# Layer 0's stores moved to ScalarE's queue, its loads alone on SyncE's, and four engines in the order of the source

## The chip, the cores and the metric

The kernel runs on one core of a Trainium2 chip. The metric is the time of one execution on the device in microseconds. Before the change it is 5983.85 us in the median of three executions (5970.71, 5983.85 and 6056.45).

## The reference, cut to what matters

The input is `x` of shape (4, 128, 64, 64): four images, 128 channels, 4096 positions. Four layers follow; the change concerns the first two.

Layer 0 is a selective scan (Mamba) over the 4096 positions of an image, with 256 inner channels `d` and 16 states `n`:

```
xs, zg = split(x projected twice)              # 256 + 256 channels
xc     = silu(conv4(xs) + conv_b)              # causal, 4 taps
dt, B, C = split(xc @ x_proj_w.T)              # 8 + 16 + 16
delta  = softplus(dt @ dt_proj_w.T + dt_proj_b)
h[d,n] = exp(delta[d] * A[d,n]) * h[d,n] + delta[d] * xc[d] * B[n]     # along the positions
y[d]   = sum_n h[d,n] * C[n] + xc[d] * D[d]
out    = (y * silu(zg)) @ out_proj_w.T + x
```

Layer 1 normalises this in groups, builds for each image a 4096 x 4096 matrix of zeros and ones (distance between two positions under 16), multiplies projected features with it twice, each time divided by the row's count of ones, and applies a batch norm over all images. Layers 2 and 3 are attention and a mixture of experts.

## The kernel before

**Layer 0** is tiled into chunks of 512 positions: 4 images (batches) of 8 chunks, 32 in all. The 256 x 16 pairs of channel and state lie on 128 partitions as 32 channels x 4 states, so a chunk has 16 steps. A step treats 2 x 32 channels and 4 states: `h` (0 or 1) is the half of the channels, `k` (0 or 1) the pair of 32-channel groups in it, and `q` (0 to 3) the group of states. Step `n` of a chunk has h = n // 8, q = n // 2 % 4, k = n % 2.

To bring delta and the product delta * xc, which lie as channels on partitions, to this layout, the kernel stores them to DRAM and reads them back four times over. `delta` (lines 222 to 245) makes `dl` and `dx`, and stores them in 16 DMAs of 32 rows x 512 values (64 KB) into four DRAM tiles `dd0` to `dd3`. `spread` (line 264) loads one of them as `r`, 128 partitions x 8 KB, with a source pattern of (4 copies, step 0) x (32 rows) x (2048 values). `small` (lines 212 to 220) makes B and C and stores them as `bcd`; `rates` (line 274) loads eight rows of it as `bt`, 128 partitions x 4 KB, with a source pattern of 4 x (32 copies, step 0) x 1024 values. A chunk has 4 loads of `r` and 8 of `bt`. Both have three buffers.

A step (lines 277 to 317) is:

- POOL: `db = r[dx] * bt[B]` (L289);
- ScalarE: two decays `hs = exp(r[delta] * A)` into PSUM (L295);
- DVE: two scans (L297), which need `hs` and `db`, and the `carry` of the chunk before;
- ScalarE: copy of the last column into `carry` (L300);
- DVE or, where (step number) % 3 is 1, POOL: `hc = h * bt[C]` (L302);
- PE, every second step: the sum over states, `y`, by products with `fold` (L308);
- after q = 3, DVE and POOL: `xc = (xc * D + y) * zs` (L314, L317).

Beside these steps stand, for the next chunk, the load of `xt` (L199, L201), the convolution as eight matmuls (`project`, L209, L210), `small`, `delta`, for this one the gate (`gate`, L254, L255), and for the last one the output projection (`after`, L325 to L328), which stores `x1` to DRAM.

**Layer 1** of a batch (`layer1`, from line 364) needs the whole batch of `x1`. It runs while layer 0 of the next batch does: `layer1` is a generator which yields after each portion of PE work, and the loop in lines 565 to 604 takes as many portions after each step as an even spread needs. It makes the 0/1 matrix in 8 panels `inc` (`compare`, L438, L441, and, for the mirrored part, `turn`, L451, L454, with loads `piece`, L491), multiplies by it (`edges`, L461 to L475), stores six of the panels to DRAM (L522), loads them again (`inc_v`, L533), multiplies once more (L548), and stores the result `hg` (L557). Batch 3 has no layer 0 beside it.

**The order of the work.** On each engine, instructions run one after the other. Which one comes first is decided by a scheduler, which walks through the source, takes what is ready by its own cost estimates and places it on the instruction's engine. Buffers of a pool are handed out in turn, and an instruction that needs a buffer waits until its last reader is done. All loads and stores of layers 0 and 1 are issued by SyncE, in one queue: a store that waits for its data keeps the loads behind it from being issued.

Of the kernel before, what the change touches and what calls it, by code (L numbers as in the profile page):

```python
# [38 lines left out]
class Net:  # L39
# [33 lines left out]
    def layers01(self):  # L73
        nc, tc, a = self.nc, self.tc, self.a
        DS, DR, T = 16, 8, CH
        NT = N // T
        HALF = 16.0 * 16.0 / 4.0
        TOP = 2.0**14
        with ExitStack() as ctx:
            wp = ctx.enter_context(tc.tile_pool(name="aw", bufs=1))  # L80
            hps = ctx.enter_context(tc.tile_pool(name="l0h", bufs=2, space=PSUM))
            yps = ctx.enter_context(tc.tile_pool(name="l0y", bufs=1, space=PSUM))
            ps = ctx.enter_context(tc.tile_pool(name="aps", bufs=3, space=PSUM))
# [8 lines left out]
            A = wp.tile([P, 8, DS], F32, tag="A", name="A")  # L92
# [13 lines left out]
            with tc.tile_pool(name="l0t", bufs=2) as tp0:  # L106
# [15 lines left out]

                for i in range(4):
                    nc.scalar.dma_start(
                        A[32 * i : 32 * i + 32, :, :], a["L0_conv_A_log"].rearrange("(k p) n -> p k n", p=32)
                    )
# [63 lines left out]
            def before(b, c):  # L190

                s = dict(b=b, c=c)
                t0 = c * T

                def load():
                    xt = s["xt"] = w2.tile([P, T + 3], F32, tag="xt", name="xt")
                    if c == 0:
                        nc.vector.memset(xt[:, 0:3], 0.0)
                        nc.sync.dma_start(xt[:, 3:], a["x"][b, :, 0:T])  # L199
                    else:  # L200
                        nc.sync.dma_start(xt, a["x"][b, :, t0 - 3 : t0 + T])  # L201

                def project():
                    xt = s["xt"]
                    xc = s["xc"] = w2.tile([P, 2, T], F32, tag="xc", name="xc")
                    for h in range(2):
                        pc = ps.tile([P, T], F32, tag="ps", name="ps_c")
                        for j in range(4):
                            nc.tensor.matmul(pc, wc[:, h, j, :], xt[:, j : j + T], start=j == 0, stop=j == 3)  # L209
                        nc.scalar.activation(xc[:, h, :], pc, AF.Silu, bias=vec[:, h, 4:5])  # L210

                def small():
                    xc = s["xc"]
                    xd = s["xd"] = w2.tile([40, T], F32, tag="xd", name="xd", bufs=1)
                    px = ps.tile([P, T], F32, tag="ps", name="ps_xd")
                    for h in range(2):
                        nc.tensor.matmul(px[:40, :], xpT[:, h, :], xc[:, h, :], start=h == 0, stop=h == 1)
                    nc.scalar.copy(xd, px[:40, :])  # L218
                    bcd = s["bcd"] = dp.tile([2 * DS, T], F32, tag="bcd", name="bcd")
                    nc.sync.dma_start(bcd, xd[DR:40, :])  # L220

                def delta():

                    xd = s["xd"]
                    dl = w2.tile([P, 2, T], F32, tag="dl", name="dl", bufs=1)
                    sp = w2.tile([P, 2, T], F32, tag="sp", name="sp", bufs=1)
                    for h in range(2):
                        pd = ps.tile([P, T], F32, tag="ps", name="ps_d")
                        nc.tensor.matmul(pd, dtT[:, h, :], xd[0:DR, :], start=True, stop=True)
                        nc.scalar.activation(sp[:, h, :], pd, AF.Abs, bias=vec[:, h, 5:6])  # L230
                        nc.scalar.activation(dl[:, h, :], pd, AF.Relu, bias=vec[:, h, 5:6])
                    nc.scalar.activation(sp, sp, AF.Exp, scale=-1.0)
                    nc.scalar.activation(sp, sp, AF.Ln, bias=1.0)
                    nc.vector.tensor_tensor(dl, dl, sp, ALU.add)
                    dx = sp
                    nc.gpsimd.tensor_tensor(dx, dl, s["xc"], ALU.mult)

                    dd = s["dd"] = [
                        dp.tile([32, 2, 2, T], F32, tag=f"dd{k}", name=f"dd{k}") for k in range(4)
                    ]  # L240
                    for k in range(4):
                        for i, t in enumerate((dl, dx)):
                            for j in range(2):
                                p0 = 64 * (k % 2) + 32 * j
                                nc.sync.dma_start(dd[k][:, i, j, :], t[p0 : p0 + 32, k // 2, :])

                return s, [load, project, small, delta]

            def gate(s):

                zs = s["zs"] = w2.tile([P, 2, T], F32, tag="zs", name="zs", bufs=1)
                for h in range(2):
                    pz = ps.tile([P, T], F32, tag="ps", name="ps_z")
                    nc.tensor.matmul(pz, wz[:, h, :], s["xt"][:, 3:], start=True, stop=True)  # L254
                    nc.scalar.activation(zs[:, h, :], pz, AF.Silu)  # L255

            def spread(s, k):

                r = w2.tile([P, 2, 2, T], F32, tag="r", name="r", bufs=3)
                dd = s["dd"][k]  # L260
                rows = bass.AP(
                    tensor=dd.tensor, offset=dd[0:1, 0, 0, :].offset, ap=[[0, 4], [4 * T, 32], [1, 4 * T]]
                )
                nc.sync.dma_start(r.rearrange("p i j t -> p (i j t)"), rows)
                return r

            def rates(s, q):
# [7 lines left out]
                return bt  # L275

            def step(s, h, q, k):


                c = s["c"]  # L280
                i = (8 * h + 2 * q + k) % 3
                if q == 0:
                    s["r"][2 * h + k] = spread(s, 2 * h + k)
                if k == 0:
                    s["bt"] = rates(s, q)
                    s["hc"] = []
                r, bt = s["r"][2 * h + k], s["bt"]
                db = w2.tile([P, 2, T], F32, tag="db", name="db")
                nc.gpsimd.tensor_tensor(db, r[:, 1, :, :], bc(bt[:, 0, :], 2), ALU.mult)  # L289
                hs = hps.tile([P, 2, T], F32, tag="hs", name="hs")  # L290
                pool = i == 1
                ho = w2.tile([P, 2, T], F32, tag="ho", name="ho", bufs=1) if pool else hs
                for j in range(2):
                    kk = 4 * h + 2 * k + j
                    nc.scalar.activation(hs[:, j, :], r[:, 0, j, :], AF.Exp, scale=Ar[:, kk, q : q + 1])  # L295
                    init = 0.0 if c == 0 else carry[:, q, kk : kk + 1]
                    nc.vector.tensor_tensor_scan(ho[:, j, :], hs[:, j, :], db[:, j, :], init, ALU.mult, ALU.add)  # L297
                if c < NT - 1:
                    kk = 4 * h + 2 * k
                    nc.scalar.copy(carry[:, q, kk : kk + 2], ho[:, :, T - 1])  # L300
                hc = w2.tile([P, 2, T], F32, tag="hc", name="hc", bufs=4)
                (nc.gpsimd if pool else nc.vector).tensor_tensor(hc, ho, bc(bt[:, 1, :], 2), ALU.mult)  # L302
                s["hc"].append(hc)
                if k == 1:
                    if q == 0:
                        s["y"] = yps.tile([P, T], F32, tag="y", name="y")
                    for j in range(4):
                        nc.tensor.matmul(  # L308
                            s["y"][32 * j : 32 * j + 32, :], fold, s["hc"][j // 2][:, j % 2, :],
                            start=q == 0, stop=q == 3, skip_group_check=True,  # L310
                        )
                    if q == 3:
                        xc = s["xc"]
                        nc.vector.scalar_tensor_tensor(  # L314
                            xc[:, h, :], xc[:, h, :], vec[:, h, 6:7], s["y"], ALU.mult, ALU.add
                        )
                        nc.gpsimd.tensor_tensor(xc[:, h, :], xc[:, h, :], s["zs"][:, h, :], ALU.mult)  # L317

            def after(s):

                b, c, xc = s["b"], s["c"], s["xc"]
                x1 = w2.tile([P, T], F32, tag="x1", name="x1", bufs=1)
                po = ps.tile([P, T], F32, tag="ps", name="ps_o")
                for h in range(2):
                    nc.tensor.matmul(po, opT[:, h, :], xc[:, h, :], start=h == 0, stop=h == 1)  # L325
                nc.vector.tensor_tensor(x1, po, s["xt"][:, 3:], ALU.add)
                nc.vector.bn_stats(self.stats[:, b, c, :], x1)
                nc.sync.dma_start(self.x1[b][:, c * T : (c + 1) * T], x1)  # L328

            def layer0():  # L330
# [267 lines left out]
            for _ in l1:  # L598
                pass
# [483 lines left out]
```

## Time and profile before

The profiled execution took 6020.19 us; its span, from the first to the last instruction, is 6018.1 us, with a mean granted clock of TensorE of 0.80.

| engine | busy us | share of the span |
|---|---|---|
| PE (matmul) | 4147.3 | 69% |
| PE weight load | 2108.1 | 35% |
| DVE | 3034.5 | 50% |
| ScalarE | 2058.3 | 34% |
| POOL | 1982.1 | 33% |

The shares are means over stages with different limits. The first decay (L295) starts at 81.3 us and the last one at 4089.7; the first one of the second batch starts at 939.1. So batch 0 of layer 0 is alone from 81 to 939 us, layer 0 of batches 1 to 3 runs beside layer 1 of batches 0 to 2 up to 4090, and layer 1 of batch 3 is alone from about 4110 to 4562. A chunk has 32 decays; counted by these it takes about 109 us in the first stage, after a first chunk of 90, and 131 us in the mean in the second. The rest is layers 2 and 3.

| DMA issue | count | KB each |
|---|---|---|
| `r <- dd` | 128 | 1024 |
| `bt <- bcd` | 256 | 512 |
| `dd <- dl`, `dd <- sp` (which holds dx) | 256 + 256 | 64 |
| `bcd <- xd` | 32 | 64 |
| `x1` stores, `hg` stores | 32 + 32 | 256 |
| `inc` stores, `inc_v` loads | 24 + 24 | 2048 |

How to read the profile's lines: a group's line gives the source line, engine, operation, output and inputs, then the count, the busy time, the mean duration in ns, and the idle time of the engine just before, with what ended it. In the waits, three numbers follow a pair: microseconds in total, times, and the longest one. SyncE computes nothing; its waits are those of its DMA queue.

### The profile page before, as it was taken

Reading aid. Unit: us, or ns where it says so; the run is one execution under the profiler, and the core shown is the slowest. Engines: PE = TensorE matmul, PEld = TensorE weight load, DVE = VectorE, ACT = ScalarE, POOL = GpSimd, SP = SyncE. Lnnn points to the kernel's source line nnn. Section 1 sums busy time; section 2 is a strip of 40 time slices with the busy share of each in tenths; the row PEclk is TensorE's granted clock in tenths of the full one; section 3 lists DMA queues with packets and bytes.
Section 4 is the critical chain, followed back from the end, with each engine's and each line's share of the span. In section 5 each row is a group of like instructions: output and inputs, shape, how many; then the busy total and the mean of one; then the engine's idle time right before and its main releaser. Section 6 shows DMA issues by size and latency. Waiting matters only on the chain. (4 is left out here: it accounts for less than half of the span.)

```text
span 6018.1 us, 52668 instructions
## 1 busy us (share of the span) xinstructions
PE 4147.3 (69%) x19383; PEld 2108.1 (35%) x19383; DVE 3034.5 (50%) x4661; ACT 2058.3 (34%) x3467; POOL 1982.1 (33%) x1076
## 2 busy tenths in 40 slices
PE   4343345778676677766677786668996666689879
PEld 1010002233332223333232333325653555357645
DVE  3555555666543566554356665435413545528631
ACT  3333334335432434443243344322323333312220
POOL 2444445344454435445354444442013000000000
PEclk6665566998888789888879897878997888769985
DMA  2222222233334223333432333341224000060042
GB/s 82 95 91 89 99 95 85 98 115 126 113 108 136 90 104 114 121 110 105 124 99 97 115 125 110 107 130 60 88 88 160 1 0 1 1 226 2 1 161 93
DMA packets 168612, 566.49 MB, mean 94 GB/s; under 512 B 20730, under 2 KB 23330, under 8 KB 145826
## 3 DMA queue, kind: packets, MB, share of 16 engines
q1 hardware_dynamic: 162386, 554.20, 26.7%
q10 hardware_dynamic: 5968, 8.93, 0.5%
q8 instruction: 152, 2.49, 0.2%
q14 instruction: 106, 0.87, 0.0%
HBM read 451.91 MB, written 111.15 MB: 94 GB/s over the span
## 5 line engine op out<-in xcount | busy, mean ns | idle before, releaser
L289 POOL TENSOR_TENSOR db<-r,bt 128x1024 f32<-128x1024 f32 x512 | 1199.7, 2350 | 1425.1 <-DMA r<-dd 674.9
L295 ACT ACTIVATE hs<-r,Ar 128x512 f32<-128x512 f32 x1024 | 704.1, 691 | 1629.3 <-DMA r<-dd 646.1
L297 DVE TENSOR_TENSOR_SCAN hs<-hs,carry,db 128x512 f32<-128x512 f32 x616 | 783.5, 1282 | 913.6 <-POOL db L289 600.6
L308 PE MATMUL y<-hc,fold 128*32 128x512 f32 x2048 | 613.6, 743 | 537.1 <-DVE hc L302 365.6
L438 PE MATMUL ps_g<-xn 128*128 128x512 f32 x1152 | 630.2, 652 | 122.9 <-DVE inc L441 84.5
L461 PE MATMUL ps_ed<-xs,inc 128*128 128x258 f16 x4096 | 590.4, 286 | 17.7 <-ACT inc L454 14.2
L461 PEld LDWEIGHTS <-inc 128*128 128x128 fp8e4 x4096 | 406.2, 102 | 334.7 <-issue 280.2
L441 DVE SCALAR_TENSOR_TENSOR inc<-ps_g,hcl,hb 128x512 fp8e4<-128x512 f32 x576 | 421.8, 741 | 193.6 <-PE ps_g L438 185.7
L302 DVE TENSOR_TENSOR hc<-hs,bt 128x1024 f32<-128x1024 f32 x352 | 425.0, 1213 | 183.9 <-ACT carry L300 164.7
L302 POOL TENSOR_TENSOR hc<-ho,bt 128x1024 f32<-128x1024 f32 x160 | 375.9, 2349 | 358.8 <-DVE ho L297 290.5
L297 DVE TENSOR_TENSOR_SCAN ho<-hs,carry,db 128x512 f32<-128x512 f32 x280 | 355.7, 1270 | 148.0 <-POOL db L289 125.1
L548 PE MATMUL ps_v<-inc_v,es 128*128 128x512 fp8e4 x1536 | 377.9, 403 | 21.2 <-ACT xd L218 21.2
L308 PEld LDWEIGHTS y<-hc,fold 128*32 128x32 f32 x2048 | 76.7, 118 | 888.2 <-DVE hc L302 327.6
L209 PE MATMUL ps_c<-xt,wc 128*128 128x512 f32 x512 | 279.3, 696 | 121.4 <-DMA xt<-in_x 118.1
L454 ACT CAST inc<-ps_tu 128x512 fp8e4<-128x512 f32 x448 | 253.7, 585 | 179.9 <-PE ps_tu L451 178.8
L438 PEld LDWEIGHTS ps_g<-xn 128*128 128x128 f32 x1152 | 194.8, 199 | 334.8 <-DVE inc L441 168.2
L548 PEld LDWEIGHTS <-es 128*128 128x128 f16 x2048 | 205.7, 102 | 292.6 <-issue 91.5
L325 PE MATMUL ps_o<-xc,opT 128*128 128x512 f32 x128 | 95.7, 860 | 255.8 <-POOL xc L317 242.3
L451 PE MATMUL ps_tu<-id,piece 128*128 128x128 fp8e4 x1344 | 138.1, 231 | 150.5 <-ACT inc L454 77.1
L209 PEld LDWEIGHTS ps_c<-xt,wc 128*128 128x128 f32 x512 | 106.9, 220 | 294.9 <-issue 189.6
L451 PEld LDWEIGHTS <-piece 128*128 128x128 fp8e4 x1344 | 106.9, 103 | 232.7 <-issue 203.7
L709 PE MATMUL ps_qkT<-cst,qkv 128*128 128x128 f32 x256 | 62.2, 423 | 150.5 <-DVE qkv L703 150.5
(261 smaller groups left out, 5677.6 us busy)
## 6 DMA issues: line engine op xcount, KB each, us to landing
bt<-bcd SPq DMA_DIRECT2D x256, 512.0 KB
r<-dd SPq DMA_DIRECT2D x128, 1024.0 KB
inc<-inc SPq DMA_DIRECT2D x24, 2048.0 KB
inc_v<-inc SPq DMA_DIRECT2D x24, 2048.0 KB
w<-in_L_ffn_weight SPq DMA_DIRECT2D x32, 1024.0 KB
w2f<-in_L_ffn_weight SPq DMA_DIRECT2D x32, 1024.0 KB
piece<-inc SPq DMA_DIRECT2D x84, 256.0 KB
dd<-dl SPq DMA_DIRECT2D x256, 64.0 KB
```

The costliest lines, as they stand in the source:

```text
L209: nc.tensor.matmul(pc, wc[:, h, j, :], xt[:, j : j + T], start=j == 0, stop=j == 3)
L289: nc.gpsimd.tensor_tensor(db, r[:, 1, :, :], bc(bt[:, 0, :], 2), ALU.mult)
L295: nc.scalar.activation(hs[:, j, :], r[:, 0, j, :], AF.Exp, scale=Ar[:, kk, q : q + 1])
L297: nc.vector.tensor_tensor_scan(ho[:, j, :], hs[:, j, :], db[:, j, :], init, ALU.mult, ALU.add)
L302: (nc.gpsimd if pool else nc.vector).tensor_tensor(hc, ho, bc(bt[:, 1, :], 2), ALU.mult)
L308: nc.tensor.matmul(s["y"][32 * j : 32 * j + 32, :], fold, s["hc"][j // 2][:, j % 2, :], start=q == 0, stop=q == 3, skip_group_check=True,)
L438: nc.tensor.matmul(pq, xn[v // 4][:, v % 4 * P : (v % 4 + 1) * P], xn[c], start=True, stop=True)
L441: nc.vector.scalar_tensor_tensor(inc[:, v, :], pq, hc[:, v : v + 1], hb, ALU.subtract, ALU.is_gt, saturate=False)
L451: nc.tensor.matmul(pt[:, i * P : (i + 1) * P], src[:, i, w * P : (w + 1) * P], id8, start=True, stop=True)
L454: nc.scalar.copy(inc[:, v, :], pt, saturate=False)
L461: nc.tensor.matmul(pe[:, : 2 * P + 2], inc[:, v, i * P : (i + 1) * P], xs[:, v, :], start=v == 0, stop=v == NB - 1,)
L548: nc.tensor.matmul(pv, es[:, e, k, :], inc[:, e, :], start=e == 0 and k == 0, stop=e == NB - 1 and k == 1,)
```

## The change

In layers 0 and 1 every store is issued by ScalarE: `bcd`, `dd`, `x1`, `inc` and `hg`. SyncE issues loads alone.

The tiles `dd0` to `dd3` become two, one for each half `h`, and each of them is stored by four DMAs of 64 rows (128 KB), two 32-row groups `j` at once, where there were eight of 32 rows. Delta is made in two halves, each in its own steps. The sum for delta moves from DVE to POOL. The pattern of the loads `r` and `bt` stays, and so do their three buffers.

The step is cut into parts, and a `slot` i issues parts of different steps: `gains` (db) and `decays` of step i + 1, `carries` of step i - 1, the scans of step i, POOL's `reads` (hc) of step i - 1, the sums of step i - 2, and the loads `r` and `bt` of steps i + 4 and i + 5. POOL takes `hc` in every second step after batch 0. The work for the next chunk stands in slots 3 to 10. The whole runs in a block in which the order on PE, ScalarE, SyncE and POOL is that of the source; DVE's is left to the scheduler.

In layer 1 the parts behind a product (`inc` copies, splits, stores) are put off by some portions (`defer`, `tick`), the panels `inc_v` are loaded in four pieces and one step ahead, the four products for `rb` become one, the pieces for `turn` are loaded ahead, and portions are taken at an even rate over three batches. The square root of the group norm is made with Ln and Exp.

```diff
-                    bcd = s["bcd"] = dp.tile([2 * DS, T], F32, tag="bcd", name="bcd")
-                    nc.sync.dma_start(bcd, xd[DR:40, :])
+                bcd = s["bcd"] = dp.tile([2 * DS, T], F32, tag="bcd", name="bcd")
+                nc.scalar.dma_start(bcd, xd[DR:40, :])
...
-                    nc.vector.tensor_tensor(dl, dl, sp, ALU.add)
-                    dx = sp
-                    nc.gpsimd.tensor_tensor(dx, dl, s["xc"], ALU.mult)
-                    dd = s["dd"] = [
-                        dp.tile([32, 2, 2, T], F32, tag=f"dd{k}", name=f"dd{k}") for k in range(4)
-                    ]
-                    for k in range(4):
-                        for i, t in enumerate((dl, dx)):
-                            for j in range(2):
-                                p0 = 64 * (k % 2) + 32 * j
-                                nc.sync.dma_start(dd[k][:, i, j, :], t[p0 : p0 + 32, k // 2, :])
+                    s["dd"] = [dp.tile([2, 32, 2, 2, T], F32, tag=f"dd{k}", name=f"dd{k}") for k in range(2)]
...
+            def delta_rest(s, h):
+                dl, sp = s["dl", h], s["sp", h]
+                nc.gpsimd.tensor_tensor(dl, dl, sp, ALU.add)
+                nc.gpsimd.tensor_tensor(sp, dl, s["xc"][:, h, :], ALU.mult)
+
+            def delta_store(s, h):
+                for i, t in enumerate((s["dl", h], s["sp", h])):
+                    for k in range(2):
+                        nc.scalar.dma_start(
+                            s["dd"][h][k, :, i, :, :].rearrange("c j t -> j c t"), t[64 * k : 64 * k + 64, :]
+                        )
...
+            def pooled(g):
+                return g % 2 == 1 if g >= SN else g % 3 == 1
...
+            def slot(i):
...
+                if n == 0 and nxt:
+                    load(nxt)
+                go(gains, i + 1)
+                go(carries, i - 1)
+                go(decays, i + 1)
+                if 0 <= i < LAST:
+                    scans(i)
+                if 0 <= i - 1 < LAST and pooled(i - 1):
+                    reads(i - 1)
+                go(sums, i - 2)
+                if i % 2:
+                    go(fetch_r, i + 4)
+                    go(fetch_r, i + 5)
+                go(fetch_bt, i + 4)
...
+                    elif n == 7:
+                        small_copy(nxt)
+                        delta(nxt, 0)
+                    elif n == 8:
+                        delta_rest(nxt, 0)
+                        delta_store(nxt, 0)
+                    elif n == 9:
+                        delta(nxt, 1)
+                    elif n == 10:
+                        delta_rest(nxt, 1)
+                        delta_store(nxt, 1)
...
+            with tc.manual_schedule(engines={mybir.EngineType.PE, mybir.EngineType.Activation, mybir.EngineType.SP, mybir.EngineType.Pool}):
```

## The prediction

> **What bounds the kernel now.** I first asked where the span goes. Layer 0 runs from 81 to 4090 us, layer 1 of the last batch alone from 4110 to 4562, and from there on the changed source is the old one. The windows view, by stage; columns are stretch, length, busy time of PE, PEld, DVE, ACT and POOL, granted clock, mean share of the 16 DMA engines, GB/s. The first three rows are three chunks of batch 0:
>
> ```profile
> core 0: us, PE busy (x) PEld busy (x) DVE busy (x) ACT busy (x) POOL busy (x), PEclk, DMA share, GB/s
> 501.00:611.40 110.40, 42.35 (x98) 8.74 (x96) 57.04 (x48) 38.75 (x65) 53.69 (x24) 0.61 0.26 93
> 611.40:721.00 109.60, 41.51 (x98) 8.75 (x96) 56.90 (x48) 38.84 (x65) 53.68 (x24) 0.59 0.27 94
> 721.00:828.50 107.50, 42.42 (x102) 8.94 (x100) 57.17 (x49) 38.86 (x66) 53.69 (x24) 0.60 0.26 96
> 172.00:939.00 767.00, 295.47 (x672) 61.62 (x668) 397.06 (x337) 268.93 (x438) 373.38 (x167) 0.60 0.27 93
> ...
> 939.00:4090.00 3151.00, 2256.65 (x9659) 1000.07 (x9660) 1735.23 (x1865) 1227.35 (x2116) 1452.51 (x765) 0.84 0.33 111
> 4110.00:4562.00 452.00, 429.17 (x2484) 265.60 (x2484) 146.74 (x243) 106.92 (x201) 54.94 (x65) 0.96 0.23 86
> ```
>
> In a chunk of batch 0 (109.2 us in the mean) no engine is busy for more than 57 us. With layer 1 beside it a chunk takes 3151/24 = 131.3 us, and PE is busy 72%. So no compute engine is the bound before 4090 us. The waits view says what is:
>
> ```profile
> DVE hs L297 <- POOL db L289: 701.3, 167, 32.9
> POOL db L289 <- DMA r<-dd: 674.9, 76, 28.0
> ACT hs L295 <- DMA r<-dd: 646.1, 85, 17.8
> ...
> POOL db L289 <- DMA bt<-bcd: 350.9, 79, 11.9
> ```
>
> The scan waits for POOL, and POOL and ACT wait for the loads r and bt. Why are these late? Part of it is SyncE's queue, which runs in order. Its own waits (all of the span):
>
> ```profile
> SPq L274 <- DVE hc L302: 830.2, 112, 22.5
> SPq L274 <- POOL hc L302: 474.3, 73, 25.8
> SPq L328 <- DVE x L326: 375.8, 32, 26.8
> SPq L264 <- ACT hs L295: 373.4, 57, 18.8
> SPq L245 <- DVE dl L234: 333.1, 29, 21.8
> ```
>
> The x1 store (L328) and the delta stores (L245) hold the queue 709 us while loads stand behind them. Lines 274 and 264 wait for a buffer to come free. The other part shows only when single transfers are windowed, same columns: an r load alone, the slowest kind of r load, the delta stores, and the output stores at the end.
>
> ```profile
> 640.00:644.50 4.50, 0.00 (x0) 0.00 (x0) 4.50 (x5) 1.61 (x5) 3.60 (x2) 0.50 0.25 106
> ...
> 668.00:679.00 11.00, 3.72 (x9) 0.33 (x8) 5.67 (x6) 4.00 (x8) 3.89 (x2) 0.58 0.25 69
> ...
> 697.00:701.80 4.80, 1.91 (x8) 0.34 (x8) 2.76 (x3) 1.64 (x4) 4.30 (x2) 0.50 0.56 142
> ...
> 5900.00:6000.00 100.00, 100.00 (x251) 56.80 (x250) 8.99 (x13) 7.03 (x12) 0.00 (x0) 0.50 0.17 65
> ```
>
> A share of 0.25 while r flows means that exactly four of the sixteen engines work, at 106 GB/s together. The source pattern of r and bt leads with a count of 4 (lines 264 and 274). The delta stores, 32 rows each, reach 0.56. So a mean share of 0.27 isn't a quarter-used DMA but four nearly full engines and twelve idle ones.
>
> **How full the four are.** The three chunk rows have a mean share of 0.263, the long row 0.27; I take 0.267, and 0.267 x 16 x 109.2 us = 466 engine-us. A chunk moves 94 GB/s x 109.2 us = 10.3 MB, of which four r of 1 MiB and eight bt of 0.5 MiB (the page's DMA issues) are 8.4 MB on the four engines. Of the other 1.9 MB, 1.05 MB are delta stores, at 142/(0.56 x 16) = 15.8 GB/s an engine 66 engine-us; 0.86 MB at the output row's 65/(0.17 x 16) = 23.9 GB/s are 36. So r and bt hold each of the four for (466 - 102)/4 = 91 us, spread traffic adds 102/16 = 6.4: 97 of 109 us. Beside layer 1: 0.33 x 16 x 131.3 = 693 engine-us; with the same 91 us the rest is (693 - 364)/16 = 20.6: 112 of 131 us. What better order can win before 4090 us is the idle rest: 12 x 8 + 19.7 x 24 = 570 us.
>
> **The change, part by part.** *Loads ahead, stores on ScalarE's queue.* The stores' 709 us leave SyncE's queue. The buffers are as many as before (three r, three bt), so lines 264 and 274's waits stay. With a load queued behind a load nearly always, I leave the engines 5% idle where it was 11 and 15%. No row shows that share; the ends are 0 and 8%.
>
> *The delta stores' shape.* Sixteen stores of 32 rows a chunk become eight of 64 rows, 128 KB each, and the destination is now written with a leading count of 2 (j), 32 (c), row. The rows give four engines for a count of 4 and over half of sixteen for 32; extended to 2, that is two engines. No row has a 2, so the ends are two and sixteen; I take two, next to the row with 4. Then each of two engines gets 8 x 64 KiB = 0.52 MB a chunk: at the output row's 23.9 GB/s 22 us, at the delta row's 15.8 GB/s 33 us. I take 25, near the first: 32 rows follow each other on an engine, as in long stores, where the old ones had two. I take it that these two are among the four of r and bt; the row 697:701.8 can't tell.
>
> The Trainium skill states a rule that bears on this, in "DMA: Bandwidth & Descriptors", section "Why a DMA increments its semaphore by 16 and not by 1": the number of engines is the largest up to 16 that divides the slowest dimension of both patterns, and the sync and scalar queues take the lowest-numbered ones. The 0.25 of r agrees with 4; for the stores the rule gives two engines, which r and bt use too, and the sum would be the one below. The same page ("Issuing engines are not separate DMA queues") says that another issuing engine saves issue time and adds no bandwidth, which speaks against the first half of the change. No run so far shows either for these stores.
>
> *Sum for the two engines.* r and bt: 91 us as now, 79 at 106 GB/s throughout. The slow r of the row at 69 GB/s was issued at 665.8 us with nothing queued ahead, which should get rarer; I take 88. Spread traffic without the old delta stores: 6.4 - 4.1 = 2.3, beside layer 1 20.6 - 4.1 = 16.5. Batch 0: 88 + 2.3 + 25 = 115.3, over 0.95 = 121.4 us a chunk, +12.2. Later: 88 + 16.5 + 25 = 129.5, over 0.95 = 136.3, +5.0. Together 8 x 12.2 + 24 x 5.0 = **+218 us**. In other words: 21 us more of stores in each of 32 chunks (+669), 355 of the 570 idle us won, 96 us of loads.
>
> *Parts at nothing,* each with its cover. The delta add goes from DVE to POOL, and in later batches POOL takes every second hc, not every third in a chunk: 16 db and 8 hc of 2.35 us, four delta products and sums and two gate products of 1.27 us are 64 of 131 us. Cover gone, POOL would need two such chunks side by side. ScalarE gains ten issues a chunk; SyncE's stores take 0.42 us each, so 4 us beside 39 to 51 busy us. ScalarE's table loads go from 239 to 232. The single rb product for four, the smaller pool work for dg (605 ns each) and the split silu lie inside PE's 28% of free time. A DMA issue on ScalarE waits for POOL's product; behind it stand the carry copy and the two decays of the next step, for which the scan waits; decays are one step ahead, and a step has 7 to 8 us. Stage 4110 to 4562: PE is busy 95%, so I leave it as it is.
>
> **Sum.** The profiled execution took 6020 us, 36 over the median 5984. 6020 + 218 - 36 = 6202, so **6200 us**. This kernel can't tell less than about 2% from no change (5864 to 6104).
>
> **Rivals.** *Spread stores* (faster): the stores use sixteen engines, or two that r and bt don't use. Then 88 + 6.4 = 94.4 and 88 + 20.6 = 108.6, over 0.93 (a shallower backlog idles more) 101.5 and 116.8: -7.7 x 8 - 14.5 x 24 = -410, 5574 us. For it: that 32 rows had over half of the engines. Against: r and bt, 128 destination rows, have four. It decides from four engines on: 12.5 us instead of 25 gives 108.2 and 123.2, -203, 5780 us.
>
> *ScalarE held by its own stores* (slower still). SyncE's issue of an r load takes 0.5 us and, behind unfinished loads, 9.8 us (the timeline at 502.95). Four stores in a row on two engines may hold ScalarE as long, twice a chunk; if half of 2 x 9.8 us isn't hidden, 32 x 9.8 = +314 more, 6516 us. Against: two engines full of backlog have work meanwhile, so part of this would be paid already.
>
> *Source order loses what the scheduler had*: PE, in source order, waits for hc with layer-1 products behind. PE has 28% free in the stage, so this would have to take 36 us of a chunk before it counts; I fold it into the one before.
>
> **Chances.** Two shared engines as summed 0.66, its own range 5950 to 6480 (loads 83 to 91, stores 22 to 33, idle 2 to 7%). Spread stores 0.20. ScalarE held 0.14. Within the first, 0.69 lies over 6104, 0.27 within 2% and 0.04 below; of the second 0.02 of 0.20 falls within 2%. So faster 0.21, same 0.20, slower 0.59. The range of 5700 to 6500 leaves out most of the second case and part of the third.
>
> **What would show it.** Right: the DMA share while dd is stored beside no other transfer is near 0.12; a chunk of batch 0 takes 115 to 126 us with POOL and ACT still waiting for r and bt; SyncE's waits for DVE and POOL at the stores are gone, waits for dd's landing are new. Spread: share far over 0.25 during the stores, chunks near 101 us. ScalarE held: its store issues take many us, and DVE waits for decays more than for db. Wrong altogether: layer 1 alone taking over 452 us, or a PE-bound middle with clock near 1.

## The result, and the profile after

The changed kernel takes **6300.39 us** in the median of three executions (6284.32 to 6350.35), 1.051 times the kernel before (95% interval 1.035 to 1.067). The forecast was 6200 in a range of 5700 to 6500: direction and range held, and the loss is about half as large again as the one forecast (+316 us on the medians, +216 forecast). The profiled execution took 6300.39 us, its span is 6298.6 us, the mean granted clock 0.775. This ratio and all later ones leave out executions that took over 1.5% longer than the fastest one of the same kernel.

Counted by the decays, as before:

| stretch of the span | before, us | after, us | difference |
|---|---|---|---|
| up to the first decay | 81.3 | 79.6 | -2 |
| batch 0: first chunk | 90 | 118 | +28 |
| batch 0: the other seven, each | 109.7 | 114.2 | +4.5 each, +32 |
| batches 1 to 3: 24 chunks, each | 131.3 | 140.9 | +9.6 each, +231 |
| from the last decay to the end | 1928.4 | 1919.6 | -9 |

These make the +280 us of the span. The windows view of the changed kernel, columns as before (stretch, length, busy time of PE, PEld, DVE, ACT and POOL, granted clock, share of the 16 DMA engines, GB/s): batch 0, batches 1 to 3, layer 1 of batch 3; then one chunk of batch 0, nine microseconds in which delta stores are the only transfer, and four in which they run beside a load of bt.

```profile
198.00:997.00 799.00, 263.45 (x676) 59.21 (x670) 383.14 (x327) 278.64 (x461) 398.17 (x191) 0.59 0.24 88
997.00:4379.00 3382.00, 2134.33 (x9402) 987.33 (x9403) 1624.90 (x1763) 1235.53 (x2173) 1629.73 (x827) 0.79 0.30 102
4400.00:4882.00 482.00, 452.29 (x2570) 269.76 (x2565) 150.50 (x245) 109.64 (x206) 49.08 (x44) 0.95 0.25 90
...
655.70:766.70 111.00, 39.84 (x96) 8.20 (x94) 53.92 (x47) 39.84 (x68) 56.30 (x27) 0.61 0.25 91
...
1486.00:1495.00 9.00, 5.73 (x20) 1.92 (x20) 5.33 (x8) 2.10 (x5) 2.18 (x2) 0.81 0.13 44
736.00:740.00 4.00, 0.00 (x0) 0.00 (x0) 0.00 (x0) 0.00 (x0) 0.00 (x0) 0.50 0.13 51
```

The DMA view of those last four microseconds, by queue (packets, MB, share of 16 engines); q10 is ScalarE's queue, q1 SyncE's:

```profile
q10 hardware_dynamic: 53, 0.10, 6.7%
q1 hardware_dynamic: 26, 0.10, 6.0%
```

The row at 1486 us is the one the forecast asked for. Stores alone have a share of 0.13, two engines of sixteen, and 44 GB/s. Counted from the packets (256 of 2 KB on each of the two, 0.088 us each) a chunk's stores take 22.5 us there. The row at 736 us shows that the two are shared: again two engines work, and both queues' packets are in flight, half the time each. The trace doesn't name the engine of a packet, but of the two packets in flight at times both are stores (28% of the four microseconds), at times both are loads (27%), at times there is one of each (38%), so neither queue has an engine to itself. The loads are the rest of a bt; in the five microseconds before, up to four of SyncE's packets were in flight at once. No compute engine does anything in these four microseconds. The mean share in batch 0 went down, from 0.27 to 0.24, though the fullest engines got more to do: the chunk became longer, and a store packet shorter (22 GB/s an engine here, 15.8 in the old shape). So the mean share says nothing of the fullest engines.

The waits of the changed kernel (engine, line, what it waits for; us in total, times, longest):

```profile
PEld y L358 <- POOL hc L347: 721.7, 76, 28.4
ACT inc L552 <- PE ps_tu L549: 637.3, 241, 26.7
PE y L358 <- POOL hc L347: 628.6, 69, 26.7
POOL db L315 <- DMA r<-dd: 584.2, 58, 20.0
...
ACT hs L323 <- DMA r<-dd: 354.9, 40, 17.1
ACT sp L257 <- DMA dd<-sp: 354.8, 29, 21.6
POOL db L315 <- DMA bt<-bcd: 327.9, 63, 16.1
```

POOL and ScalarE still wait for r and bt, as before. PE's wait for POOL's hc (L347) has grown from 169.9 to 628.6 us. New is that ScalarE waits 355 us at L257 until its own stores of the product have landed. SyncE's own waits, same columns:

```profile
SPq L292 <- POOL hc L347: 2409.5, 198, 29.2
...
SPq L282 <- ACT hs L323: 380.5, 72, 20.1
...
SPq L292 <- DVE hc L347: 332.6, 54, 25.1
SPq L282 <- DMA dd<-sp: 155.5, 18, 33.4
```

The stores are gone from here, and loads of r that wait for dd to land are new. In their place the load of bt (L292) stands 2410 us at the head of the queue, waiting for POOL's hc, which reads one of bt's three buffers; before, it waited 474 us for POOL's hc and 830 for DVE's. The loads of r (L282) are queued behind it.

### The profile page after: what moved, and what is told of

Same layout as the page of the kernel before. It is cut to its first block, busy times and chain, and to the rows that moved or that the text cites. A ratio compares the mean times of both kernels' runs of the same rounds, so it can differ in the third digit from the quotient of the medians.

```text
span 6298.6 us, 52346 instructions
## 1 busy us (share of the span) xinstructions
PE 3969.0 (63%) x19191; PEld 2074.4 (33%) x19191; DVE 2912.6 (46%) x4550; ACT 2085.4 (33%) x3560; POOL 2190.2 (35%) x1151
## 5 line engine op out<-in xcount | busy, mean ns | idle before, releaser
L358 PE MATMUL y<-hc,fold 128*32 128x512 f32 x2048 | 457.3, 773 | 822.0 <-POOL hc L347 628.6
L333 DVE TENSOR_TENSOR_SCAN hs<-hs,carry,db 128x512 f32<-128x512 f32 x484 | 622.4, 1287 | 569.4 <-ACT hs L323 247.8
L536 PE MATMUL ps_g<-xn 128*128 128x512 f32 x1152 | 668.4, 688 | 297.2 <-ACT inc L552 108.5
L333 DVE TENSOR_TENSOR_SCAN ho<-hs,carry,db 128x512 f32<-128x512 f32 x412 | 509.5, 1269 | 500.3 <-ACT hs L323 240.5
L347 POOL TENSOR_TENSOR hc<-ho,bt 128x1024 f32<-128x1024 f32 x235 | 551.8, 2348 | 36.1 <-PE y L358 34.7
L347 DVE TENSOR_TENSOR hc<-hs,bt 128x1024 f32<-128x1024 f32 x277 | 337.4, 1218 | 7.2
L207 PE MATMUL ps_c<-xt,wc 128*128 128x512 f32 x512 | 237.8, 608 | 3.1 <-DMA xt<-in_x 3.1
L264 POOL TENSOR_TENSOR dl<-dl,sp 128x512 f32<-128x512 f32 x64 | 80.8, 1263 | 356.1 <-ACT sp L260 230.9
L257 ACT ACTIVATE sp<-ps_d,vec 128x512 f32<-128x512 f32 x64 | 44.0, 687 | 466.2 <-DMA dd<-sp 354.8
L368 POOL TENSOR_TENSOR xc<-xc,zs 128x512 f32<-128x512 f32 x64 | 80.9, 1265 | 266.6 <-DVE xc L365 262.6
```

The source lines that it names most:

```text
L333: nc.vector.tensor_tensor_scan(ho[:, j, :], hs[:, j, :], st["db"][:, j, :], init, ALU.mult, ALU.add)
L347: (nc.gpsimd if pooled(g) else nc.vector).tensor_tensor(hc, st["ho"], bc(s["bt"][h, q][:, 1, :], 2), ALU.mult)
L358: nc.tensor.matmul(s["y"][32 * j : 32 * j + 32, :], fold, steps[g - 1 + j // 2]["hc"][:, j % 2, :], start=q == 0, stop=q == 3, skip_group_ ...
L536: nc.tensor.matmul(pq, s.xn[v // 4][:, v % 4 * P : (v % 4 + 1) * P], s.xn[c], start=True, stop=True)
```

## The experiments

The names in the expectations: T1, two DMA engines carry r, bt and all delta stores, and this sets the time; T2, ScalarE is held by its own stores; T3, the order of the source costs time; T4, bt's buffers are held by POOL's hc; T5, the order on ScalarE and PE. Ratios are to the kernel before, run beside it on the same chip, with a 95% interval. The changed kernel's own ratio is known to 1.6% only, so a gain of 2.7% over it is just outside of what can be told.

### The stores' shape, alone and undone

The changed kernel with stores of 32 rows again, sixteen a chunk, still on ScalarE (e1_32row_stores):

```diff
-                        nc.scalar.dma_start(
-                            s["dd"][h][k, :, i, :, :].rearrange("c j t -> j c t"), t[64 * k : 64 * k + 64, :]
-                        )
+                        for j in range(2):
+                            p0 = 64 * k + 32 * j
+                            nc.scalar.dma_start(s["dd"][h][k, :, i, j, :], t[p0 : p0 + 32, :])
```

> The changed kernel with the delta stores as before: 16 a chunk, 32 rows each, still issued by ScalarE. Theory 1 (two DMA engines carry r, bt and all delta stores, and their load sets the time): the prediction's own sum for spread stores, 101.5 us a chunk in batch 0 and 116.8 later, about 5570 us. Theory 2 (ScalarE is held by its own stores, 355 us waiting for landings and some 270 us in issues that don't come through): both waits go, half of them on the path, about 5980 us. Theory 3 (the source's order costs the time, whatever the stores look like): about 6300 us, as the changed kernel.

The kernel before with the new shape and nothing else, eight stores of 64 rows on SyncE (e6_before_64row):

```diff
-                            for j in range(2):
-                                p0 = 64 * (k % 2) + 32 * j
-                                nc.sync.dma_start(dd[k][:, i, j, :], t[p0 : p0 + 32, k // 2, :])
+                            p0 = 64 * (k % 2)
+                            nc.sync.dma_start(
+                                dd[k][:, i, :, :].rearrange("c j t -> j c t"), t[p0 : p0 + 64, k // 2, :]
+                            )
```

> The kernel before with only the delta stores changed: 8 a chunk, 64 rows each with a leading count of 2, still issued by SyncE. Theory 1: 21 us more a chunk on two of the four engines, of which the idle 12 us (batch 0) and 20 us (later) take a part: 100 to 350 us slower, 6080 to 6330 us. Theory 2: no store is on ScalarE, within 1% of before. Theory 3: the same as before.

The shape alone, in the old order, costs 273 us: 6269.83 us, 1.046 (1.039 to 1.052). Undone in the new order, it gives back 161 us only: 6139.69 us, 1.024 (1.018 to 1.030). The windows of batch 0 and of batches 1 to 3, first with the shape alone, then with it undone:

```profile
190.00:1017.00 827.00, 317.61 (x676) 62.22 (x676) 400.42 (x339) 269.79 (x440) 373.62 (x168) 0.58 0.23 87
1017.00:4382.00 3365.00, 2218.62 (x9656) 995.69 (x9657) 1740.17 (x1865) 1234.75 (x2122) 1449.57 (x765) 0.82 0.29 104
```

```profile
182.00:919.00 737.00, 268.31 (x676) 60.32 (x668) 383.11 (x327) 277.88 (x461) 397.86 (x192) 0.59 0.28 96
919.00:4217.00 3298.00, 2131.92 (x9402) 991.21 (x9403) 1623.78 (x1763) 1234.53 (x2173) 1629.62 (x827) 0.79 0.32 105
```

So the two-engine stores are a cause, and a large one; e6 came out as T1 expected, while e1 fits no theory by itself. But the changed kernel without them isn't the 5574 us of the rival "spread stores": chunks of batches 1 to 3 still take 137.4 us, against 131.3 before. Counted from the packets, no DMA engine at all moves anything for 17% of that stretch; it was 9% in the changed kernel and 10.6% before. I call this the idle share from here on. It is a lower limit for the engines that carry r and bt, since a transfer on other engines alone counts as busy. The order of the loads has lost something too.

### The loads cut to use all engines

r and bt each in four DMAs of 32 partitions, without the leading count of 4; in the changed kernel (e2_loads_on_16) and in the kernel before (e3_before_loads_on_16). Shown for r, bt likewise:

```diff
-                    ... ap=[[0, 4], [4 * T, 32], [1, 4 * T]]
+                    ... ap=[[4 * T, 32], [1, 4 * T]]
-                nc.sync.dma_start(r.rearrange("p i j t -> p (i j t)"), rows)
+                for i in range(4):
+                    nc.sync.dma_start(r[32 * i : 32 * i + 32].rearrange("p i j t -> p (i j t)"), rows)
```

> The changed kernel with each load of r and bt cut into four of 32 partitions, whose source pattern leads with 32. By the rows of the kernel before such a shape gets more than half of the sixteen engines. Theory 1: r and bt take 88 x 4 / 16 = 22 us of an engine a chunk, the DMA is no bound any more, and POOL (64 of 141 us) and PE (some 90 of 141 us busy) are next: 5200 us or less. Theory 2: ScalarE's stores land sooner, but still on two engines: 5900 to 6100 us. Theory 3: as the changed kernel.

> The kernel before with the loads of r and bt cut into four of 32 partitions, as in the changed kernel's run at 5391 us; all else as before. Theory 1 (four engines set the time before the change too): 5400 to 5600 us. If the old order were bound by its own waits instead, r and bt would come only some 10 us sooner each, and it would stay above 5800 us.

The changed kernel falls to 5390.98 us, 0.899 (0.891 to 0.907); the kernel before only to 5859.1, 0.977 (0.971 to 0.984). The windows of the first (batch 0, batches 1 to 3), and then the longest waits of the second in its batches 1 to 3:

```profile
163.00:756.00 593.00, 261.91 (x678) 58.49 (x672) 386.51 (x329) 277.50 (x461) 398.46 (x191) 0.63 0.45 119
756.00:3447.00 2691.00, 2027.77 (x9396) 962.62 (x9397) 1624.23 (x1762) 1235.66 (x2172) 1631.79 (x829) 0.86 0.45 129
```

```profile
ACT hs L298 <- DVE hs L300: 541.1, 203, 14.6
POOL hc L305 <- DVE ho L300: 540.5, 99, 17.6
PEld y L311 <- DVE hc L305: 473.0, 138, 16.5
PE y L311 <- DVE hc L305: 451.6, 98, 15.6
```

T1 had expected 5200 or less of the first and 5400 to 5600 of the second; it has the direction of both and the size of neither, and for the second the other case that was named, above 5800, came out. Still, 909 us go with one edit that leaves every compute engine's work as it was: the four engines were the bound of the changed kernel. In the kernel before, the loads nearly leave the list of waits (POOL's wait for bt at db falls from 351 to 148 us, that for r from 675 to none) and the steps wait for one another instead (decays for the scans before them, POOL and PE for DVE). A chunk of batch 0 gets some 17 us shorter, the later ones hardly any (in a profiled execution of 5924 us, the longest of the six). There the old order is a second limit, close behind the first: 132.9 us a chunk against 112.1 in the new order. So the new order, with the rest of the change, is the better one; little of what it wins is had while four engines carry the loads.

### Who holds SyncE's queue

In batches 1 to 3 POOL does hc in the odd steps. The odd step is the last reader of its bt, and POOL issues its hc (2.35 us) a slot later than DVE would (1.22 us). So hc was swapped: POOL in the even steps, DVE in the odd. Once in the changed kernel (e7_after_hc_swapped), once with the 32-row stores too (e9_32row_hc_swapped).

```diff
-                return g % 2 == 1 if g >= SN else g % 3 == 1
+                return g % 2 == 0 if g >= SN else g % 3 == 1
```

> The changed kernel with this swap alone; the stores stay at 64 rows. Theory 4 and theory 1 together: the two engines with stores are nearer their bound here (idle 9%), so it gains less, 6150 to 6260 us. Theory 5: within 1% of the changed kernel's 6300 us.

> The 32-row stores on ScalarE again (6140 us), and after batch 0 POOL takes the hc of the even steps in place of the odd ones, as many as before. A bt is read by an even and an odd step, and its buffer is free after the odd one's hc: on DVE this comes in the slot after the even step's on POOL, not a slot later. Theory 4 (with the stores spread, what is left of the loss is that SyncE's queue waits for POOL's hc before it may load the next bt, 1845 us of waits after 919 us, with the r loads behind it, and the four engines then stand idle 17% of the time against 10% before the change): the idle falls to about 10%, 5870 to 6000 us. Theory 5 (the idle comes from the order on ScalarE and PE, not from bt's buffer): within 1% of 6140 us.

Measured: 6134.68 us, 1.025 (1.018 to 1.032), and 5906.62 us, 0.984 (0.978 to 0.991), 166 and 233 us less than without the swap. The first is a little more than expected, the second as expected. SyncE's waits in batches 1 to 3, first with 32-row stores alone, then with the swap:

```profile
SPq L292 <- POOL hc L347: 1844.8, 174, 31.8
SPq L282 <- ACT hs L323: 366.8, 50, 24.2
```

```profile
SPq L292 <- DVE hc L347: 1299.5, 140, 20.2
SPq L282 <- ACT hs L323: 421.6, 45, 25.1
SPq L292 <- POOL hc L347: 199.1, 60, 18.8
```

1845 us at POOL's hc (and 9 at DVE's) become 1499 at both engines'. The idle share goes from 17% of the stretch to 8.5%, and with the 64-row stores from 9% to 4%; batch 0, where the edit changes nothing, stays at 114 and 106 us a chunk. This is the wait that keeps the loads from being as far ahead as their places in the source say. That the swap helps by serving PE sooner is not what the waits show: PE's weight loads wait 606 us for POOL's hc without the swap and 607 with it (all of the span, 32-row stores). With 32-row stores and the swap together the changed kernel is no longer slower than the kernel before (0.984), so undoing these two is enough to undo the whole loss.

### The place of the second half's stores, and ScalarE

Delta's second half is made in slots 9 and 10, right behind the first; both use one buffer. The timeline of ScalarE in the changed kernel (start, length, engine, line, operation, and in brackets the wait before it with what ended it):

```profile
722.91 1.03 ACTq L271 DMA_DIRECT2D dd<-sp  x2
723.98 0.19 ACT L341 COPY carry<-ho 128x2 f32<-128x2 f32 x1 [3.38 <-DMA dd<-sp]
724.08 1.41 ACT L323 ACTIVATE hs<-r,Ar 128x512 f32<-128x512 f32 x2
742.93 0.69 ACT L257 ACTIVATE sp<-ps_d,vec 128x512 f32<-128x512 f32 x1 [17.44 <-DMA dd<-sp]
```

L257 would overwrite what the first half's stores are still reading, and waits 17 us until they have landed; decays and carries stand behind it. Three edits of slots: both parts of the second half three slots later, with the 64-row stores (e4_second_half_later) and with 32-row stores (e14_32row_later), and only the stores later, with 32 rows (e15_32row_late_store). The diff is that of e4 and e14; in e15 `delta_store` alone goes to slot 13.

```diff
-                    elif n == 9:
+                    elif n == 12:
                         delta(nxt, 1)
-                    elif n == 10:
+                    elif n == 13:
                         delta_rest(nxt, 1)
                         delta_store(nxt, 1)
```

In e4 and e14 the slots run from below zero, so the first chunk's second half is made and stored twice, and the first decay comes at 118.5 and 100.2 us, not at 79.6; what is gained later is gained in spite of this.

> The changed kernel with the second half of delta made in slot 12 and stored in slot 13, where it was 9 and 10. ScalarE then has three more steps before it writes over what the first half's stores still read. Theory 1: the bytes on the two engines are the same, 6240 to 6360 us. Theory 2: most of the 355 us of ScalarE's wait for the stores' landing goes, 5950 to 6100 us. Theory 3: as the changed kernel.

> The 32-row stores on ScalarE and the second half of delta in slots 12 and 13. Either change alone took some 165 us off the changed kernel. Theory 2 (the later half helps because ScalarE no longer waits for the first half's stores to land): with 32 rows these land soon anyway, so nothing is added, within 1% of 6140 us. If the later half helps by putting the stores' bytes elsewhere in the chunk, it helps the 32 rows too, though less: 6040 us or below.

> The 32-row stores, and of delta's second half only the stores go from slot 10 to slot 13; it is made in slots 9 and 10 as in the changed kernel. Making it in slots 12 and 13 and storing it in 13 had brought 6140 us to 5915 us. If that came from the stores' place in the chunk, this gives 5900 to 5980 us. If it came from the work of both halves no longer standing in slots 7 to 10 on ScalarE, POOL and PE, it stays within 1% of 6140 us. Between these it would be both.

Measured: 6133.99 us, 1.025 (1.018 to 1.033); 5914.91, 0.983 (0.975 to 0.992); 5969.51, 0.994 (0.991 to 0.998). With 64 rows the later half wins 166 us, between what T1 and T2 expected, and the wait at L257 falls from 355 to 144 us. That looked like proof that ScalarE's wait costs the time. It isn't: with 32-row stores this wait was 30.6 us in all, and the later half wins 225 us there. Moving the stores alone wins 170 of them. So with 32 rows the place of the stores in the chunk counts, whoever waits for them; the rest of 55 us, hardly more than the intervals can tell, goes with the place where the half is made. How much of e4's gain is ScalarE's wait isn't shown. What the stores collide with in slot 10 (the next loads of r are the likely ones) no run tells apart.

The same 64-row stores issued by SyncE (e5_dd_on_sync):

```diff
-                        nc.scalar.dma_start(
+                        nc.sync.dma_start(
```

> The changed kernel with its 64-row delta stores issued by SyncE, at the same places in the source; all other stores stay on ScalarE. Theory 1 alone (bytes on the two engines): the queue doesn't matter, within 1% of 6300 us. Theory 2: ScalarE's issues that don't come through (some 270 us) go, but loads of r and bt then stand behind stores that wait for POOL: 6150 to 6500 us, with SyncE's waits for POOL's product new.

The ratio is 1.046 (1.034 to 1.059; 6262 and 6334 us), beside 1.051 (1.035 to 1.067) on ScalarE. Which queue issues these stores makes no difference that these intervals can tell. That agrees with the Trainium skill's "DMA: Bandwidth & Descriptors" ("Issuing engines are not separate DMA queues"), which the prediction held against this half of the change; the other stores were not moved back.

### All limits lifted

The changed kernel with cut loads and 32-row stores (e12_both_spread), and with the hc swap besides (e13_both_spread_swapped); the diffs are those shown above.

> The changed kernel with the 32-row stores and the loads cut into four. Theory 1: the stores are off the two engines too; ScalarE's 282 us of wait for their landing go, half of it on the path, 5200 to 5300 us. Theory 2 says the same here. If the new order is worth anything, it ends below the kernel before with cut loads.

> Stores of 32 rows, loads cut into four, and the swap of hc between POOL and DVE after batch 0, all three. With the DMA no longer the bound, bt's buffer matters less than at 6140 us, where the swap won 233 us: 4950 to 5065 us.

Measured: 5064.86 us, 0.846 (0.840 to 0.853), and **5049.61 us, 0.838 (0.831 to 0.844)**, 16% under the kernel before and the fastest version of all; e12 is faster than the 5200 to 5300 us expected, e13 within its range. The windows of batch 0 and of batches 1 to 3, of e12 and then of e13, and ahead of them three microseconds of e12 in which loads, nearly all of them r, are the only transfer:

```profile
511.00:514.00 3.00, 3.00 (x8) 1.33 (x7) 2.77 (x4) 0.00 (x0) 0.80 (x2) 1.00 1.03 218
...
137.00:632.00 495.00, 262.58 (x678) 59.95 (x676) 384.15 (x329) 277.44 (x463) 398.86 (x192) 0.66 0.57 143
632.00:3158.00 2526.00, 2016.22 (x9402) 952.62 (x9401) 1624.63 (x1763) 1233.58 (x2173) 1631.26 (x829) 0.88 0.49 137
```

```profile
138.00:633.00 495.00, 263.60 (x678) 60.06 (x674) 383.61 (x328) 277.26 (x463) 398.58 (x192) 0.65 0.57 142
633.00:3082.00 2449.00, 1986.52 (x9417) 947.60 (x9418) 1629.54 (x1763) 1229.95 (x2172) 1633.78 (x829) 0.89 0.51 141
```

In e13 a chunk takes 71 us in batch 0 and 102 later. POOL is now busy 81% of batch 0 (399 of 495 us) and PE 81% of batches 1 to 3 (1987 of 2449): in these two stages no run but e12 comes near this. With the DMA limit gone the swap, worth 166 to 233 us before, is worth 15 in the median, less than the intervals can tell. In SyncE's queue 801 us at DVE's hc and 249 at POOL's remain in front of bt, but POOL waits only 77 us for r and 31 for bt.

## Why the prediction was right, and where it was wrong

| term, us a chunk | forecast | measured |
|---|---|---|
| stores on two engines | 25 | 22.5 |
| r and bt, mean of all | 88 | 91 |
| fullest engines busy, batch 0 | 115.3 | 112.0 |
| fullest engines busy, later | 129.5 | 127.9 |
| idle, batch 0 | 5% | 2% |
| idle, later | 5% | 9% |
| chunk, batch 0 | 121.4 | 114.2 |
| chunk, later | 136.3 | 140.9 |

(Busy is here the measured chunk less the idle share, which is the time without any DMA packet; so it is an upper limit for the fullest engines, and idle a lower one. Stores and loads are sums of packet times; packets on one engine overlap a little, so they add up to some per cent more than the busy time.)

**Four engines carry the loads: right,** shown by e2. **Two engines carry the new stores, and they are shared with the loads: right,** shown by the two rows of 0.13, by e6 (+273 us) and by e1 (-161 us). That they are shared had been an assumption; the row at 736 us shows it. **The work on these engines was summed well:** 113 us a chunk for stores and loads, 113.5 measured. In part that is luck, since two small errors are opposite: the loads didn't get shorter as the forecast argued (91 us, 90 before by the same count).

**Wrong: "with a load queued behind a load nearly always, I leave the engines 5% idle".** This one share for both stages is the step that failed. In batch 0 it was too pessimistic, and the forecast was 38 us too high there; in batches 1 to 3 too optimistic, and it was 111 us too low; that the total is nearer than that is luck too. Counted from the packets the old kernel idled 9.5% in batch 0 and 10.6% later (I had worked out 11 and 15% for the four engines), and the change brought this to 2% and 9%: of this idle time hardly any was won in batches 1 to 3, where most of the gain was forecast. The row that spoke against it was among those shown of before: SyncE waiting 830 and 474 us at line 274 for hc, on DVE and on POOL. I had noted that the three buffers of bt stay, and then drew nothing from it. The issue distance of four steps that the source writes down isn't had with three buffers when the last reader of one is put off by a slot.

**Wrong: POOL's part "at nothing".** I counted POOL's busy time (64 of 131 us) and found room. But an engine that isn't full can still hold a buffer: POOL's hc in every odd step frees bt later, and SyncE's queue stood behind it. The swap, which leaves POOL's work the same, wins 166 us (e7) or 233 us (e9).

**Wrong: ScalarE's wait as hidden.** I named the wait for POOL's product, and waits for landing only as a sign, but not that both halves of delta share a buffer, so that ScalarE also waits until the stores have landed: 355 us in all. Nor are the issues free. The group of these stores, of the changed kernel (shortest, median and longest issue in ns, then the first and the last start in us):

```profile
L271 ACTq DMA_DIRECT2D dd<-dl x128: 487/503/1284, 46.7 to 4231.6; - x128
L271 ACTq DMA_DIRECT2D dd<-sp x128: 487/589/13557, 48.4 to 4232.7; - x128
```

Half of them take 0.5 or 0.6 us at most; the longest took 13.6. The 256 sum to 402 us, some 270 more than at half a microsecond each, near the 314 us that the rival "ScalarE held" put down. So what it described exists. But it isn't shown to set the time: with the issues on SyncE (e5) the ratio is the same within the intervals, and in e1, where the wait for landing is nearly gone, the later half still wins 225 us. Its other sign, DVE waiting more for decays than for db, didn't come: 529 us against 626.

**The rival "spread stores"** had its mechanism right and its size wrong: 6140 us measured for 5574. It took the loads' backlog as given, and idle 7%, where it was 17% later. With the hc swap, which brings the idle share down to 8.5%, it is 5907, and with the second half later 5915; the two weren't tried together.

**The 570 us of idle time as what better order can win** stands as an upper end only: the best without cut loads (e9, e14) is 1.6 to 1.7% under the kernel before, 95 to 100 us.

**The other signs.** A chunk of batch 0 takes 114.2 us, just under the 115 to 126 named. "Layer 1 alone taking over 452 us" was named as a sign of being wrong altogether, and it came: the row from 4400 us has 482. From the last decay to the last product of layer 1 it is some 34 us more (502 against 468), and what follows takes 43 us less, so none of the 280 us lies there, and the sign was badly chosen. Why layer 1 alone got longer is open.

## What to carry to other kernels

A low mean DMA share isn't a DMA with room to spare: window one transfer alone, multiply its share by 16, and see how many engines carry it; then sum the work of the fullest engines, not of all. This counts engines only while the transfer keeps them busy: in the 4.8 us of the old delta stores with a share of 0.56, ten stores of 64 KB were issued, 137 GB/s, about what was moved (142), so there the pace of the issues, and not the number of engines, seems to set the share. A reordering pays what the tightest resource allows: this one lost 5% on two to four engines and won 15% (e12) once loads and stores were spread over many more by nothing but the shape of their patterns. For every load that is to run ahead, look for the last reader of its buffer, on whichever engine, since the queue behind it waits for that reader and not for the distance written in the source.

## What the runs showed that I had not expected

- Cutting a broadcast load of a leading count of 4 into four DMAs of 32 partitions puts it on all engines, but each is then slower: all sixteen busy (a share of 1.03, since packets overlap) at 218 GB/s in the window of e12, where a whole r ran at 0.25 and 106 GB/s in the kernel before. That is twice the rate and not four times: 13.6 GB/s an engine against 26.5.
- A small transfer in a bad shape is dear: 273 us in the old order for stores whose bytes are a tenth of a chunk's (1.05 of 10.3 MB).
- The stores' packets became faster: 15.8 GB/s an engine in the old 32-row stores, 22 (44 over two) in the 64-row ones. The old shape is slower on each engine and much better for the kernel.
